# Attention with turned heads: values formed once and reordered by DMA, and an adapter's first matmul on two column tiles of TensorE

## The chip, the cores and the metric

The kernel runs on one core of one Trainium2 chip. The metric is the device time of one execution in microseconds (us). TensorE is called PE below (its weight loads PEld), VectorE DVE, ScalarE ACT, GpSimd POOL, and SyncE, which issues all DMAs here, SP.

## The reference, cut to what matters

The batch has 8 sequences of 512 tokens with 256 features, all in fp32. Each passes an attention block with 16 heads of 16 features, a feed-forward layer, an adapter, a rotation of feature pairs, and a second adapter.

```python
x = _ln(src) * (1.0 + scale) + shift                  # per batch, from the time step
q, k, v = (heads(x @ W + b) for W, b in ((Wq, bq), (Wk, bk), (Wv, bv)))
scores = q @ k.T / sqrt(16) + attention_bias          # (8, 16, 512, 512) of bias
probs = softmax(where(src_mask, -inf, scores))
x = x + (heads_joined(probs @ v) @ Wo + bo)
x = x + gelu2((_ln(x) * g2 + beta2) @ W1 + b1) @ W2 + b2

# an adapter, twice, with a rotation between the two; A = 64
hidden = gelu(x @ down_W.T + down_b)                  # (512, 256) -> (512, 64)
hidden = hidden @ expert_W[domain].T + expert_b[domain] + domain_emb[domain]
x = layer_norm(hidden @ up_W.T + up_b + x) * gamma + beta
```

## The kernel before

**The order of the work.** The kernel does not emit instructions as its loops run. `Plan` collects tasks, each with a cost per engine, a rank, and the buffers it reads and writes. `Plan.run` then plays them through a list scheduler: an engine that is free takes the ready task of the lowest rank for which buffers are left, and the tasks are emitted in that order. Where two engines can do a task (most PSUM evictions), the one that is free first takes it. A changed cost, buffer count or dependency therefore changes the order of all engines. Each engine then runs its own instructions strictly in the emitted order; so does SP with its DMA issues.

**Stages.** `prepare(b)` loads a sequence, normalises it, transposes it to `xT` (features on partitions) and forms q, k and v. `attention(u, n)` handles one unit: a batch, a group of four heads (`g`), and a tile of 128 queries; there are 128 units. `finish(b, ts)` takes two token tiles of 128 (in the very last half of the run, one at a time) through output projection, feed-forward and both adapters. While batch b is in attention, `prepare(b + 1)` and the `finish` of earlier halves are interleaved with it by rank.

**A unit.** Four bias tiles of 128x512 are loaded (L863), POOL adds the mask (L867), PE forms scores (L875), DVE adds them to the bias tile with the row minimum (L886), ACT takes the exponential in place (L890). The probabilities then have to get keys onto the partitions. There are two ways:

- Straight heads: PE transposes four blocks (L925) and ACT or DVE evicts them (L652) to `pT`.
- Turned heads: the first `TURNED = 2` heads of a group. DVE transposes 32x32 blocks (L901) to `tb`, and a DMA of four issues (L910) brings the blocks to `pT`. In this way the keys of a block of 128 land in a turned order: partition 4r + m holds key 32m + r. `turned_groups(b)` says which groups are turned: all four, but only the last one in batch 0 and only the first three in batch 7.

The product with the values (L951) runs on four column tiles of 32, one per head of the group, with 32 columns of `v_pad` from a head's start as weights. `v_pad` holds for each token tile and head 16 features and a one, which gives the softmax's sum.

**Values in two orders.** For the turned heads the values must stand on the partitions in the turned order. Before the change, `prepare` evicts each transposed half of the sequence twice, once to `xT` and once, permuted, to one of two buffers `xTp` that it borrows from the bias buffers (L760 on ACT, L762 on DVE). Each token tile's values are then formed in parts (L810): the turned heads of every group from `xTp`, the others from `xT`. In batches 0 and 7 there are three parts, else two, with two matmuls each. DVE adds the bias (L821).

**The adapter's way down.** `adapter` transposes two token tiles, and multiplies with the 64 columns of `down_W.T` (L1059): per half of the features one matmul with 64 weight columns and 256 tokens streamed, output on 64 partitions. ACT takes the gelu (L1065) to `hid`, whose 65th row is one. `db` holds the bias per batch.

Bias buffers: 17 (`BIAS`). An fp32 matmul leaves two records of weight load and two of matmul in the trace.

Of the kernel before, what the change touches and what calls it, by code (L numbers as in the profile page):

```python
# [219 lines left out]
def conditioned_sequence_kernel(  # L220
# [45 lines left out]
    QZ = slots("qz", 2, [P, 2, NC, S])  # L266
    KT = slots("kT", 2, [P, NC, S])
    VP = slots("v_pad", 2, [P, NT * H * (HD + 1) + 32 - HD - 1])
    BIAS = slots("bias", 17, [P, S])
    LOW = slots("low", 4, [P, 4])  # L270
    PT = slots("pT", 2, [P, 4 * NT * 2 * P])
    TB = slots("tb", 2, [P, TURNED * S])
# [60 lines left out]

    def heads_of(v):

        return v[:, : NT * H * (HD + 1)].rearrange("p (t h e) -> p t h e", t=NT, h=H)

    def turned_groups(b):

# [18 lines left out]
    invalid = const.tile([A, B], F32, tag="invalid", name="invalid")  # L358
    expert_i = const.tile([1, B], I32, tag="expert_i", name="expert_i")
    ccT = const.tile([P, NC, B + 1], F32, tag="ccT", name="ccT")  # L360
    db = const.tile([A, B + 1], F32, tag="db", name="db")
    ada_rows = tc.dram_tile([B, 2 * D], F32, name="ada_rows")
    rot_rows = tc.dram_tile([B, 2 * D], F32, name="rot_rows")
    turned_rows = tc.dram_tile([B, D], F32, name="turned_rows")
# [101 lines left out]
    def constants():  # L466
        plan.rank = -13.0

        further = Buffer(BG, lambda t: t[:, :8])
        plan(PE, 0.3, lambda: nc.tensor.matmul(  # L470
            further.t, shifted[:, :P], cols[:, :8], start=True, stop=True),
            [], [further], mode="full", at=4.0)

        def biases():
            nc.vector.tensor_tensor(
                bk,
                cols[:, C_BK : C_BK + NG].rearrange("p (c u) -> p c u", u=2)[:, :, 0],
                further.t[:, 4:8].rearrange("p (c u) -> p c u", u=2)[:, :, 1],
                ALU.add,
            )  # L480

            for u, src in enumerate((cols[:, C_BQ : C_BQ + NG], further.t[:, :4])):
                nc.vector.tensor_scalar(
                    bqh[:, u], src.rearrange("p (c u) -> p c u", u=2)[:, :, u],
                    halves[:, u : u + 1], None, ALU.mult,
                )

        plan(DVE, 0.6, biases, [further], ["bk", "bqh"], at=4.2)

        for c in range(NC):  # L490
            for n, w in ((1, wq), (2, wk)):

                def dense(n=n, w=w, c=c):
                    for k in range(NC):
                        src = first[:, n, k, c * 2 * P : (c + 1) * 2 * P]
                        src = src.rearrange("p (u j e) -> p u j e", u=2, e=32)[:, :, :, :HD]
                        dst = w[:, k, c, :].rearrange("p (j u d) -> p u j d", u=2, d=HD)
                        nc.gpsimd.tensor_copy(dst, src)

                plan.rank = -9.0 + 0.1 * (n + 2 * c)  # L500
                plan(POOL, 0.55, dense, [], [("w", n, c)], at=7.5 + 1.2 * n)


        for i, v_pad in enumerate(VP.tiles):

            def clear(v_pad=v_pad):
                nc.gpsimd.memset(v_pad, 0.0)
                nc.gpsimd.memset(heads_of(v_pad)[:, :, :, HD : HD + 1], 1.0)

            plan.rank = -10.0  # L510
            plan(POOL, 2.0, clear, [], [("ones", i)])
        plan.rank = 1.0

        def later():
            for hid in HID.tiles:
                nc.gpsimd.memset(hid[A:A1, :], 1.0)

        plan(POOL, 0.6, later, [], ["hid1"])

        plan(ACT, 0.25, lambda: nc.scalar.activation(  # L520
            b1s, cols[:, C_B1 : C_B1 + NF], AF.Copy, scale=0.851), [], ["b1s"], at=4.0)
# [25 lines left out]
    def rotations():  # L547
# [88 lines left out]
        plan(PE, 0.9, hidden, ["ccT", "wd"], [hs], mode="down")  # L636

        def added():
            nc.vector.tensor_scalar(
                db[:, :B], hs.t[:, 1, :B], cols[:A, C_DB + 1 : C_DB + 2], None, ALU.add  # L640
            )
            nc.vector.tensor_scalar(
                db[:, B:], hs.t[:, 0, B:], cols[:A, C_DB : C_DB + 1], None, ALU.add
            )

        plan(DVE, 0.3, added, [hs], ["db"])


    def evict(pair, r, w, act=0.47, dve=0.6):
# [78 lines left out]
    def prepare(b):  # L728
# [8 lines left out]
                m8.t, mask[b].rearrange("(t p) k -> p t k", p=P)), [], [m8], data=1.1)  # L737
        rstd = statistics(res, rk, range(NT), at=(4.0, 4.0, 4.8, 4.8) if b == 0 else None)
        normed(lambda t: res.t[:, t, :], rk, res, rk, range(NT), rstd)
        xT, xTp = Buffer(XT), [Buffer(BIAS) for _ in range(NC)]  # L740
        for c in range(NC):
            ps = Buffer(BG)

            def turn(c=c, ps=ps):
                for t in range(NT):
                    nc.tensor.transpose(
                        ps.t[:, t * P : (t + 1) * P], res.t[:, t, c * P : (c + 1) * P], ident
                    )

            plan(PE, 0.44, turn, rk, [ps], mode="full")  # L750

            def modulated(e, place, c=c, ps=ps):

                s, t = modc[:, c, b : b + 1], modc[:, NC + c, b : b + 1]
                dst, src = xT.t[:, c, :], ps.t
                if place:
                    dst = xTp[c].t.rearrange("p (k r m) -> p k m r", k=NT, m=4)
                    src = src.rearrange("p (k m r) -> p k m r", k=NT, m=4)
                if e == ACT:
                    nc.scalar.activation(dst, src, AF.Identity, bias=t, scale=s)  # L760
                else:
                    nc.vector.tensor_scalar(dst, src, s, t, ALU.mult, ALU.add)  # L762

            for place in range(2):
                plan({ACT: 0.66, DVE: 0.72 + 0.33 * place}, 0, lambda e, place=place, m=modulated: m(e, place),
                     [ps, "modc"], [xTp[c] if place else (xT, c)])

        qz, kT, v_pad = Buffer(QZ), Buffer(KT), Buffer(VP)

        def chunk(w, c, n):  # L770
            ps = Buffer(BG)
# [12 lines left out]
        for c in range(NC):  # L784
# [6 lines left out]
            if b == 0 and c == 0:  # L791

                plan.end(-8.0, -5.0)
                plan.begin()
        bv = bv_row.rearrange("p (h d) -> p h d", h=H)
        for h in range(2):
            ps = Buffer(BG, lambda t: t.rearrange("p (i d) -> p i d", i=2))
            for i in range(2):
                t = 2 * h + i

                def sums(t=t, i=i, ps=ps):

                    t0, t1 = turned_groups(b)
                    parts = (xTp, 0, t0, t1), (xT, 1, 0, NG), (xT, 0, 0, t0), (xT, 0, t1, NG)
                    for src, u, g0, g1 in parts:
                        if g0 == g1:
                            continue
                        for c in range(NC):
                            cut = "p (g u e) -> p u g e"
                            nc.tensor.matmul(  # L810
                                ps.t[:, i, :].rearrange(cut, g=NG, u=2)[:, u, g0:g1],
                                src[c].t[:, t * P : (t + 1) * P] if src is xTp
                                else xT.t[:, c, t * P : (t + 1) * P],
                                wv[:, c, :].rearrange(cut, g=NG, u=2)[:, u, g0:g1],
                                start=(c == 0), stop=(c == NC - 1),
                            )

                plan(PE, 0.87, sums, [(xT, 0), (xT, 1), *xTp, "wv"], [(ps, i)], mode="full")
            for i in range(2):
                t = 2 * h + i  # L820
                plan(DVE, 0.335, lambda t=t, i=i, ps=ps: nc.vector.tensor_tensor(  # L821
                    heads_of(v_pad.t)[:, t, :, :HD], ps.t[:, i, :].rearrange("p (h d) -> p h d", h=H),
                    bv, ALU.add), [(ps, 0), (ps, 1), ("ones", 0), ("ones", 1), "bv"], [(v_pad, t)])
        negs = [Buffer(NEG) for _ in range(NT)]
        for t in range(NT):
            plan(ACT, 0.52, lambda t=t: nc.scalar.activation(
# [17 lines left out]
        if b == 0:  # L844
            for n, task in enumerate(plan.stream):
                task.rank = 1.0 + n
            plan.stream = None
        state[b] = (res, rk, m8, negs, qz, kT, v_pad)


    pTs, sums_of, live = {}, {}, {}
# [1 line left out]
    def attention(u, n):  # L853
        b, g, qt = u
        c, par = divmod(g, 2)
        half, i = divmod(qt, 2)
        _, _, m8, negs, qz, kT, v_pad = state[b]
        qs = slice(qt * P, (qt + 1) * P)
        plan.rank = n - 2.0

# [81 lines left out]
        def values():  # L942
            for kc in range(NT):
                for j in range(4):
                    at = (kc * H + 4 * g + j) * (HD + 1)
                    if j < turned:
                        pj = pT.t[:, : 8 * TURNED * P].rearrange(
                            "p (a h k c) -> p h k a c", a=8, h=TURNED, k=NT)[:, j, kc]
                    else:
                        pj = pT.t.rearrange("p (j k f) -> p j k f", j=4, k=NT)[:, j, kc]  # L950
                    nc.tensor.matmul(  # L951
                        pv.t[32 * j : 32 * j + 32, :], v_pad.t[:, at : at + 32],
                        pj, start=(kc == 0), stop=(kc == NT - 1),
                    )

        plan(PE, 1.77, values,
             [(v_pad, t) for t in range(NT)]
             + [(pT, a, j) for a in range(2) for j in range(turned, 4)]
             + [(pT, a) for a in range(2) if turned], [pv], mode="col")
        sb = Buffer(PVS)  # L960
# [81 lines left out]
    def adapter(b, l, res, rk, ts):  # L1042
# [9 lines left out]
            eus[l] = eu  # L1052
        eu = eus[l]
        xT, xk = half_transposed(lambda t: res.t[:, t, :], rk, ts)
        ps, hid = Buffer(BG, lambda t: t[:A, : 2 * P]), Buffer(HID)

        def down():
            for c in range(NC):
                nc.tensor.matmul(  # L1059
                    ps.t[:, :w], wd[:, l, c, :], xT.t[:, c, :w], start=(c == 0),  # L1060
                    stop=(c == NC - 1),
                )

        plan(PE, 0.05 + 0.43 * n, down, [*xk, "wd"], [ps], mode="down")
        plan(ACT, 0.15 + 0.12 * n, lambda: nc.scalar.activation(  # L1065
            hid.t[:A, :w], ps.t[:, :w], AF.Gelu, bias=db[:, b : b + 1] if l else db[:, B:]),
            [ps, "hid1", "db"], [hid], mode="gelu")

        def add(ps):
            nc.vector.tensor_tensor(res.t[:, rows], ps, res.t[:, rows], ALU.add)  # L1070
# [267 lines left out]
```

## Time and profile before

| | |
|---|---|
| median of 3 runs | 959.73 us (958.97 to 961.05) |
| the profiled execution, its time | 959.75 us |
| its span, first to last instruction | 957.9 us |
| mean granted TensorE clock | 0.987 of full |
| DMA: share of the 16 engines, moved | 71.8%, 214.25 MB |
| chain that ended last, by engine | PE 59%, ACT 12%, DVE 10%, DMA 8%, POOL 7%, issue 4% |
| L810, matmuls of the values | 288 records |
| L1059, the adapters' way down | 136 records; 128x256 form 396 ns busy each |
| L760 to the turned order, ACT | 11 of 1282 ns |
| L762 to the turned order, DVE | 5 of 1230 ns |
| L1065 gelu, ACT | 30 of 64x256 at 469 ns, 4 of 64x128 at 362 ns |

The page gives each engine's busy time, the groups of instructions by line with a mean duration and the idle time before them with what ended it, and the chain of work followed back from the last instruction. A matmul's duration in a group contains the length of the pipeline; how long PE is really taken by it is seen from the start of the next one, as in the chain in order of time.

### The profile page before, as it was taken

To read this page: it belongs to the slowest core of one execution; us is meant where nothing else is said; L and a number is where in the kernel's file an instruction comes from. 1 tells how busy PE (TensorE), PEld (TensorE's weight loads), DVE (VectorE), ACT (ScalarE), POOL (GpSimd) and SP (SyncE) were. 2 spreads that over 40 slices of the span, in tenths; PEclk is the share of its full clock that TensorE was granted. 3 is DMA by queue.
4 is the path that set the end of the run, shared out by engine and by line. 5 is a ranking of instruction groups with operands and counts; after the bars stand their busy time and mean duration, and the time that the engine had idled before them with its cause. 6 is when DMAs were issued, how large, how long until landed. Compare 5 with 4: busy or idle time off the path is not lost.

```text
span 957.9 us, 20961 instructions
## 1 busy us (share of the span) xinstructions
PE 905.7 (95%) x6646; PEld 594.7 (62%) x6646; DVE 783.4 (82%) x2142; ACT 764.8 (80%) x1379; POOL 754.1 (79%) x841
## 2 busy tenths in 40 slices
PE   7989999999999999999999999999989999899994
PEld 5646666567566765667656666567656666566782
DVE  3778788887979898988978888888888888788656
ACT  5977779787897878979797888978799786897542
POOL 7699999787877879789796878888796987888122
PEclk8999999999999999999999999999999999999997
DMA  9497495888859876797958878597775968878000
GB/s 295 151 325 230 157 318 164 269 255 243 243 168 277 273 239 194 243 283 219 305 159 261 259 224 286 159 295 260 240 239 170 292 202 261 257 219 261 11 16 23
DMA packets 158945, 214.25 MB, mean 224 GB/s; under 512 B 18479, under 2 KB 90201, under 8 KB 158834
## 3 DMA queue, kind: packets, MB, share of 16 engines
q1 hardware_dynamic: 158834, 212.91, 71.8%
q8 instruction: 53, 0.87, 0.4%
q14 instruction: 58, 0.48, 0.1%
HBM read 149.89 MB, written 4.24 MB: 161 GB/s over the span
## 4 chain that ended last, share of the span: by engine, by line
PE 59%; ACT 12%; DVE 10%; DMA 8%; POOL 7%; issue 4%; SPq 1%; POOLq 0%; DVEq 0%; ACTq 0%
PE bank L875 10%; PE bank L1031 10%; PE bank L925 9%; PE bank L951 8%; PE bank L1006 8%; DMA bias<-in_bias 7%; POOL bias L867 4%; PE bank L773 4%; ACT bias L890 3%; DVE bias L886 3%; PE bank L1059 2%; PE bank L694 2%; PE bank L718 2%; PE bank L810 2%; ACT bank L682 1%
## 5 line engine op out<-in xcount | busy, mean ns | idle before, releaser
L867 POOL TENSOR_TENSOR bias<-bias,neg 128x512 f32<-128x512 f32 x512 | 580.8, 1161 | 101.1 <-DMA bias<-in_bias 73.4
L890 ACT ACTIVATE bias<-bias,low 128x512 f32<-128x512 f32 x512 | 343.6, 719 | 74.1 <-DVE low L886 73.6
L886 DVE CUSTOM_DVE_ANT_0 bias<-bank,bias 128x512 f32<-128x512 f32 x512 | 327.8, 684 | 71.2 <-PE bank L875 63.5
L925 PE MATMUL bank<-shifted,bias 128*128 128x128 f32 x1152 | 161.7, 278 | 11.5 <-ACT pT L652 2.3
L925 PEld LDWEIGHTS bank<-shifted,bias 128*128 128x128 f32 x1152 | 128.6, 141 | 64.2 <-issue 15.0
L901 DVE STREAM_TRANSPOSE tb<-bias 128x512 f32<-128x512 f32 x224 | 148.3, 691 | 9.4 <-ACT bias L890 8.8
L875 PE MATMUL bank<-kT,qz 32*128 32x512 f32 x1024 | 152.2, 643 | 0.6 <-DVE low L886 0.6
L652 ACT COPY pT<-bank 128x512 f32<-128x512 f32 x218 | 119.6, 583 | 22.3 <-PE bank L925 21.5
L1006 PE MATMUL bank<-hT,w 128*128 128x256 f32 (+1 forms) x544 | 123.8, 371 | 3.3 <-DVE gT L1022 1.8
L951 PE MATMUL bank<-pT,v_pad 128*32 128x256 f32 x2048 | 125.0, 385 | 0.6 <-DVE res L1124 0.3
L1031 PE MATMUL bank<-w,gT 128*128 128x256 f32 x496 | 122.3, 383 | 0.0
L1006 PEld LDWEIGHTS bank<-hT,w 128*128 128x128 f32 x544 | 95.2, 190 | 26.5 <-issue 8.4
L1031 PEld LDWEIGHTS bank<-w,gT 128*128 128x128 f32 x496 | 89.6, 190 | 26.7 <-issue 14.8
L951 PEld LDWEIGHTS bank<-pT,v_pad 128*32 128x32 f32 x2048 | 60.5, 110 | 60.9 <-issue 11.8
L1018 POOL TENSOR_SCALAR sig<-sig 128x512 f32<-128x512 f32 (+1 forms) x68 | 40.2, 593 | 55.3 <-ACT sig L1015 52.5
L875 PEld LDWEIGHTS bank<-kT,qz 32*128 32x128 f32 x1024 | 43.4, 183 | 43.7 <-issue 21.5
L1022 DVE SCALAR_TENSOR_TENSOR gT<-bank,cols,sig 128x256 f32<-128x256 f32 (+1 forms) x128 | 54.3, 465 | 14.2 <-POOL sig L1018 14.1
L1015 ACT ACTIVATE sig<-bank,b1s 128x256 f32<-128x256 f32 (+1 forms) x136 | 55.7, 456 | 8.2 <-PE bank L1006 7.9
L660 DVE BATCH_NORM_STATS2 st<-res 128x6 f32<-128x256 f32 x128 | 52.4, 410 | 10.1 <-DMA res<-in_x 8.5
L652 DVE COPY pT<-bank 128x512 f32<-128x512 f32 x70 | 46.4, 680 | 5.7 <-PE bank L925 4.7
L682 ACT ACTIVATE bank<-res,rstd 128x256 f32<-128x256 f32 x64 | 36.3, 567 | 16.9 <-POOL rstd L669 15.4
L668 POOL TENSOR_TENSOR rstd<-rstd,neg_half 128x2 f32<-128x2 f32 (+2 forms) x59 | 43.4, 736 | 4.9
(145 smaller groups left out, 1117.6 us busy)
## 6 DMA issues: line engine op xcount, KB each, us to landing
bias<-in_bias SPq DMA_DIRECT2D x512, 256.0 KB, 4.3
pT<-tb SPq DMA_DIRECT2D x448, 128.0 KB, 3.6
out<-res SPq DMA_DIRECT2D x15, 256.0 KB, 3.5
res<-in_x SPq DMA_DIRECT2D x7, 512.0 KB, 4.7
m<-in_mask SPq DMA_DIRECT2D x8, 256.0 KB
mod<-ada_rows SPq DMA_DIRECT2D x8, 256.0 KB
w<-in_w SPq DMA_DIRECT2D x2, 1024.0 KB
rot<-rot_rows SPq DMA_DIRECT2D x8, 256.0 KB, 4.2
```

The costliest lines, as they stand in the source:

```text
L652: nc.scalar.copy(*pair()) if e == ACT else nc.vector.tensor_copy(*pair())), r, w)
L867: plan(POOL, 1.12, lambda j=j: nc.gpsimd.tensor_tensor(dif[j].t, dif[j].t, negs[qt].t, ALU.add), [negs[qt]], [dif[j]])
L875: nc.tensor.matmul(sc[j].t, qz.t[strip, par, c, qs], kT.t[strip, c, :], start=True, stop=True,)
L886: plan(DVE, 0.61, lambda j=j: nc.vector.tensor_tensor_reduce(dif[j].t, sc[j].t, dif[j].t, -1.0, 3.0e38, ALU.add, ALU.min, low.t[:, j : j + ...
L890: plan(ACT, 0.61, lambda j=j: nc.scalar.activation(dif[j].t, dif[j].t, AF.Exp, bias=low.t[:, j : j + 1], scale=-1.0), [(low, j)], [dif[j]] ...
L901: plan(DVE, 0.62, lambda j=j: nc.vector.transpose(tb.t.rearrange("p (m h k c) -> h p k m c", m=4, h=TURNED, k=NT)[j], dif[j].t.rearrange(" ...
L925: nc.tensor.transpose(ps.t[:, kc, :], dif[j].t[:, kc * P : (kc + 1) * P], ident)
L951: nc.tensor.matmul(pv.t[32 * j : 32 * j + 32, :], v_pad.t[:, at : at + 32], pj, start=(kc == 0), stop=(kc == NT - 1),)
L1006: nc.tensor.matmul(ps.t[:, i, :w], w1[:, c, f * P : (f + 1) * P], hT.t[:, c, :w], start=(c == 0), stop=(c == NC - 1),)
L1015: plan(ACT, 0.155 + 0.1 * n, lambda i=i, f=f, ps=ps, sg=sg: nc.scalar.activation(sg.t[:, i, :w], ps.t[:, i, :w], AF.Tanh, bias=b1s[:, f : ...
L1022: plan(DVE, 0.14 + 0.13 * n, lambda i=i, f=f, ps=ps, sg=sg: nc.vector.scalar_tensor_tensor(gT.t[:, f, :w], ps.t[:, i, :w], cols[:, C_B1 + ...
L1031: nc.tensor.matmul(ps.t[:, i, :], gT.t[:, f, i * P : (i + 1) * P], w2[:, f, :], start=(f == 0), stop=(f == NF - 1),)
```

## The change

Values are formed once per token tile, from `xT` alone, with two matmuls of 256 columns. The second, permuted eviction and the buffers `xTp` are gone. `v_pad` is laid out by the head's place in its group first, so that the part of the turned heads is one contiguous run of 544 numbers on each partition. When all four token tiles of a batch are in, SP issues four DMAs that copy that run to a new buffer `v_turn`, each from 32 neighbouring partitions to every fourth one. The values' product takes its weights of the turned heads from `v_turn`. There are two `v_turn` buffers, and 16 bias buffers instead of 17.

In the adapter, each matmul of two token tiles is cut in two of 128 tokens, the second on the array's second 64 columns, so that its output lies on partitions 64 to 127. The gelu is taken in two instructions of 64x128, the second of which reads partitions 64 to 127 and writes partitions 0 to 63. `db` is therefore formed on both halves of the partitions. The planner's cost of the way down falls from 0.91 to 0.52, that of the gelu rises from 0.39 to 0.54.

```diff
-    BIAS = slots("bias", 17, [P, S])
+    VT = slots("v_turn", 2, [P, NT * NG * TURNED * (HD + 1) + 32 - HD - 1])
+    BIAS = slots("bias", 16, [P, S])
...
-        return v[:, : NT * H * (HD + 1)].rearrange("p (t h e) -> p t h e", t=NT, h=H)
+        return v[:, : NT * H * (HD + 1)].rearrange("p (j t g e) -> p t j g e", j=4, t=NT, g=NG)
...
-            for place in range(2):
-                plan({ACT: 0.66, DVE: 0.72 + 0.33 * place}, 0, lambda e, place=place, m=modulated: m(e, place),
-                     [ps, "modc"], [xTp[c] if place else (xT, c)])
+            plan({ACT: 0.66, DVE: 0.72}, 0, modulated, [ps, "modc"], [(xT, c)])
...
-                    parts = (xTp, 0, t0, t1), (xT, 1, 0, NG), (xT, 0, 0, t0), (xT, 0, t1, NG)
...
+                    for c in range(NC):
+                        nc.tensor.matmul(
+                            ps.t[:, i, :], xT.t[:, c, t * P : (t + 1) * P], wv[:, c, :],
+                            start=(c == 0), stop=(c == NC - 1),
+                        )
...
+        def turned_values():
+            size = NT * NG * TURNED * (HD + 1)
+            to = v_turn.t.rearrange("(r m) f -> m r f", m=4)
+            for m in range(4):
+                nc.sync.dma_start(to[m, :, :size], v_pad.t[32 * m : 32 * m + 32, :size])
+
+        plan(DMA, 1.8, turned_values, [(v_pad, t) for t in range(NT)], [v_turn], data=1.0)
...
-                        pv.t[32 * j : 32 * j + 32, :], v_pad.t[:, at : at + 32],
+                        pv.t[32 * j : 32 * j + 32, :],
+                        (v_turn if j < turned else v_pad).t[:, at : at + 32],
...
         def down():
             for c in range(NC):
-                nc.tensor.matmul(
-                    ps.t[:, :w], wd[:, l, c, :], xT.t[:, c, :w], start=(c == 0),
-                    stop=(c == NC - 1),
+                for i in range(n):
+                    nc.tensor.matmul(
+                        ps.t[A * i : A * i + A], wd[:, l, c, :], xT.t[:, c, i * P : (i + 1) * P],
+                        start=(c == 0), stop=(c == NC - 1),
+                    )
+
+        def hidden():
+            for i in range(n):
+                lanes = slice(A * i, A * i + A)
+                nc.scalar.activation(
+                    hid.t[:A, i * P : (i + 1) * P], ps.t[lanes], AF.Gelu,
+                    bias=db[lanes, b : b + 1] if l else db[lanes, B:],
                 )
...
-        plan(PE, 0.05 + 0.43 * n, down, [*xk, "wd"], [ps], mode="down")
+        plan(PE, 0.52, down, [*xk, "wd"], [ps], mode="down")
+        plan(ACT, 0.27 * n, hidden, [ps, "hid1", "db"], [hid], mode="gelu")
```

The DVE addition L821 now writes 4x4x16 numbers per token tile instead of 16x16, and POOL clears the last 15 columns of both `v_turn` buffers at the start.

## The prediction

> **What bounds the kernel now.** I read the page's busy shares first, then the busy time by stage, then the chain in order of time, then the groups of the touched lines, then SP's own queue.
>
> From the page (busy us, share of the span, instructions):
>
> ```profile
> span 957.9 us, 20961 instructions
> PE 905.7 (95%) x6646; PEld 594.7 (62%) x6646; DVE 783.4 (82%) x2142; ACT 764.8 (80%) x1379; POOL 754.1 (79%) x841
> ```
>
> PE's ends are modelled, so 95% alone proves little. The busy time by stage (first number the stretch's length, then PE, PEld, DVE, ACT, POOL) shows the same in stretches of about one batch:
>
> ```profile
> 312.00:432.00 120.00, 115.03 (x866) 76.81 (x866) 106.49 (x287) 100.07 (x177) 98.56 (x106) 1.00 0.78 244
> ...
> 552.00:672.00 120.00, 116.43 (x817) 76.28 (x818) 101.61 (x279) 103.65 (x181) 98.68 (x105) 1.00 0.78 242
> ...
> 890.00:958.00 68.00, 53.33 (x348) 40.70 (x342) 41.76 (x116) 28.54 (x69) 16.95 (x42) 0.92 0.05 16
> ```
>
> In a steady batch PE lacks only 3.6 to 5 of 120 us; the next engine, DVE, lacks 13 or more. PE is the bound, at full granted clock, except at the start and in the last 40 us. What a matmul really occupies is its pitch, which the chain in order of time gives (start, length, engine, line, records; an fp32 matmul leaves two records). From the start and from batch 2:
>
> ```profile
> 28.19 1.31 PE bank L810 x12
> ```
>
> ```profile
> 182.93 0.44 PE bank L925 x4
> ...
> 191.71 1.86 PE bank L951 x32
> ...
> 199.65 0.89 PE bank L810 x8
> 200.54 0.88 PE bank L718 x4
> ...
> 213.94 1.01 PE bank L1059 x4
> ...
> 259.80 1.22 ACT bias L760
> ...
> 262.63 1.18 ACT bias L760
> ```
>
> Four records that stream 128 columns take 0.44 us (0.109 each); four of 256 columns take 0.87 to 0.88. L1059, the adapters' way down, is 0.87 plus 0.14 of changing the tiling of the array. L951 streams 256 columns on four column tiles: 32 records in 1.86 us is 58 ns each against 217 alone, so four tiles run at once at 3.7 of 4. The last two rows are the copy of the modulated rows into the turned order, on the chain.
>
> **The change part by part.**
>
> *Adapters' way down.* 30 calls on two token tiles: four records of 256 columns become eight of 128, in two column tiles of 64. If the tiles run together as in L951, that is four steps of 0.109, 0.44, and with the switch 0.58 us instead of 1.01: 0.43 saved, 30 × 0.43 = 12.9 us of PE. The four calls on one token tile keep four records of 128 columns: nothing. The weight loads decide whether this holds; in the groups (busy us, mean ns | idle before and its releasers):
>
> ```profile
> L925 PEld LDWEIGHTS bank<-shifted,bias 128*128 128x128 f32 x1152 | 128.6, 141 | 64.2 <-issue 15.0 <-ACT bias L890 11.5 <-ACT pT L652 7.1
> ...
> L951 PEld LDWEIGHTS bank<-pT,v_pad 128*32 128x32 f32 x2048 | 60.5, 110 | 60.9 <-issue 11.8 <-ACT bias L890 10.0 <-DVE res L1070 2.6
> ...
> L1059 PEld LDWEIGHTS bank<-hT,wd 128*64 128x64 f32 x136 | 16.2, 140 | 18.9 <-issue 3.3 <-DVE hT L652 3.2 <-ACT hT L652 2.5
> ```
>
> Eight loads of 140 ns now stand in four steps of 109. [...] L951's 32 loads of 110 ns are 3.5 us inside 1.86 us, on column tiles of the same rows, and L925's loads of 141 ns pass at a pitch of 109. I take 0.43 saved; [...].
>
> *Values.* Before, the four matmuls of a token tile in batches 1 to 6 take 0.89; after, two of 256 columns at L718's 0.87: 24 tiles × 0.02 = 0.5 us. In batches 0 and 7 a token tile has six matmuls, 1.31: 8 × (1.31 − 0.87) = 3.5. Together 4.0 us of PE. PE's sum is 16.9.
>
> *The turned copies go.* 11 on ACT at 1282 ns and 5 on DVE at 1230: 14.1 us of ACT and 6.2 of DVE. 8 of ACT's stand on the chain (9.7 us). They also held the PSUM bank and two bias buffers.
>
> *Gelu in two.* A 64x256 ACTIVATE is 469 ns, a 64x128 one 362 (row L1065): 30 × (2 × 362 − 469) = 7.7 us more on ACT, which still nets −6.4. The second half reads lanes 64 to 127 and writes lanes 0 to 63; no row shows such a shift, bounds 362 and 469 each, I take 362. On a layer's own chain down and gelu together are 0.43 − 0.26 = 0.17 shorter. Table loads stay at 56 in the instruction order, so the planner did not scatter the gelus; changes of PE tiling go from 397 runs to 398.
>
> *v_pad's layout.* The 32 DVE additions now write 4x4x16 instead of 16x16. Runs stay 16 elements; the row is 412 ns; a transposing one such as L762's costs 1230 against 800. Bounds 0.41 and 0.63 (the same ratio), taken 0.41: zero, and at most 7 us on DVE, which has 13 us a batch to spare. Two more 64-lane additions for db, and two POOL memsets of 15 columns at the start, are below 1 us in all, beside the start's loads.
>
> *The transfer of the turned values.* 32 DMAs of 32 partitions × 2176 B. Its nearest row is pT<-tb:
>
> ```profile
> bias<-in_bias SPq DMA_DIRECT2D x512, 256.0 KB, 4.3
> pT<-tb SPq DMA_DIRECT2D x448, 128.0 KB, 3.6
> ```
>
> Four issues of pT<-tb take 2.50 us of SP (0.62 each), so SP gets 2.5 us a batch more, and the DMA engines 2.2 MB on 214 (1%, at a share of 72%). Landing about 3.6 us. Who waits: the values' matmuls of the next batch's first head group. In the trace of before, v_pad of batches 1 to 7 is full 28 to 48 us ahead of them (batch 7: 778.1 and 819.8), and batch 0 is turned only in its fourth group (39.8 and 82.4). So 2.5 + 3.6 fits. Queued behind the wait on SP are bias loads and pT<-tb, and behind those POOL. In the changed kernel's instruction order, the bias load behind the transfer is for a buffer that DVE frees after the last v_pad write (batches 2, 4, 6, 7) or one instruction ahead of it (3); in batch 0 v_pad is done before SP gets there; only in batches 1 and 5 does SP wait for v_pad alone. So the wait is hidden by what SP waits for anyway, in its own queue:
>
> ```profile
> SPq L863 <- DVE tb L901: 86.8, 58, 7.7
> SPq L863 <- PE bank L925: 73.1, 56, 6.9
> ```
>
> If that cover is gone, a batch pays up to the 2.5 us of issue. I take nothing, with 0 and 8 × 2.5 = 20 us as bounds.
>
> *Bias buffers 17 to 16.* The two turned copies took two of 17 from the copy to the last values' matmul, 505 of 958 us, so 15 were left for half the time and 17 for the other. POOL's gaps ahead of L867 are as dense in the one (48 us in 505) as in the other (44 in 452). Nothing, from either side ±2 us.
>
> **Sum.** PE does 16.9 us less. How much reaches the end? If only the chain's PE share (59%) counted, 10; if all as in the steady stages (96%), 16. ACT and DVE, the other parts of the chain, get 6.4 and 6.2 us lighter, so I take 0.8: 13.5 us. The profiled execution takes 959.75 us (span 957.9 and 1.85 around it), the median of the runs 959.73, so both bases agree: 959.7 − 13.5 = 946.2. Planning the order anew moves unrelated waits, by a few us either way (PE's idle in a batch already differs by 1.6 us from stage to stage): own range 940 to 952.
>
> **Rivals.**
>
> *Other engines hold the end (12%).* PE gets shorter, but the loop bias load, POOL, DVE, ACT keeps its length: bias<-in_bias is 7% of the chain and POOL L867 4%. For it: POOL 99 us and DVE up to 106 of 120. Against: PE's own idle is the smallest. Half arrives: 952.
>
> *The column tiles don't run together (6%), so the change doesn't do what it says.* The call stays at 8 × 0.109 + 0.14 = 1.01. Left are the values, 4.0 × 0.8: 956.5. Against it, L951.
>
> *The transfer blocks SP (5%).* The 2.5 us of issue come on the path in half of the batches: 10 us given back, 956.
>
> *Loads are exposed (7%), the case that is slower.* Place: each way down of two token tiles. [...] It decides from the point where a call takes over 1.01 + 4.0/30 = 1.14 us, that is 70 ns exposed per load. For it: a load takes 140 ns, a step 109, and two loads fall in a step. Against: L925's and L951's pitches.
>
> **How the numbers follow.** The forecast has 70%. Faster by over 0.2% (1.9 us, about what a measurement of this kernel can tell): the forecast, the half gain, and most of the 956 cases, 0.89; within 0.2%: 0.04, the rest of those; slower 0.07. The range 939 to 956.5 takes in all but the exposed loads and the outer ends of the forecast.
>
> **What would show it.** Right: L1059's successor takes 0.58 us in the chain with both halves' records starting within some ns; 0.87 a token tile for the values in every batch; ACT and DVE each about 6 us less busy; PE busy near 889; PE's idle per batch still 3 to 5 us. SP's wait at the new transfer short or in place of a bias wait. Wrong: a way down over 0.8 us, PE's idle above 6 us per batch, L951 waiting for v_turn, or POOL's wait for bias loads well over 73 us.

## The result, and the profile after

The changed kernel takes 949.96 us (median of 14 runs, 944.99 to 957.14) against 959.6 us of the kernel before beside it (14 runs): a ratio of 0.9888, interval 0.9861 to 0.9916. That is 10.7 us by the ratio, which compares runs taken side by side, and 9.6 between the medians. The profiled execution took 954.41 us, the second longest of its runs, at a mean granted clock of 0.977 (before: 0.987).

The page of the changed kernel: span, busy time of each engine, and the chain by engine.

```profile
span 952.6 us, 20975 instructions
...
PE 901.4 (95%) x6606; PEld 595.6 (63%) x6606; DVE 785.1 (82%) x2143; ACT 760.7 (80%) x1394; POOL 754.5 (79%) x843
...
PE 53%; ACT 20%; DVE 9%; DMA 9%; issue 4%; SPq 2%; POOL 2%; DVEq 0%; POOLq 0%; ACTq 0%
```

PE is busy 4.3 us less, not 16.9, and its idle time is 51.2 us against 52.2. Part of this is the clock. In some stretches the granted clock is 0.50; counted as span × (1 − granted clock), this half clock cost 12.5 us in the profiled execution before and 21.9 us in this one, so at full clock PE would be about 13.7 us less busy (an estimate from these two and the 4.3). On the chain PE's share went from 59% to 53% and ACT's from 12% to 20%. The stretches of one batch (length, then PE, PEld, DVE, ACT, POOL, granted clock, DMA share, GB/s):

```profile
312.00:432.00 120.00, 114.31 (x860) 75.77 (x859) 105.56 (x286) 101.00 (x182) 99.92 (x110) 0.99 0.77 244
552.00:672.00 120.00, 117.34 (x875) 76.17 (x873) 104.12 (x283) 103.79 (x186) 98.78 (x106) 1.00 0.78 245
885.00:953.00 68.00, 54.49 (x369) 43.75 (x368) 41.53 (x113) 31.52 (x79) 17.64 (x43) 0.87 0.05 17
```

PE lacks 5.7 us in the one and 2.7 us in the other. The two edited stages, in the chain in order of time (start, length, engine, line, records):

```profile
197.19 0.59 PE bank L1062 x8
197.78 0.59 PE bank L700 x4
198.37 0.87 PE bank L925 x8
199.24 0.87 PE bank L803 x4
```

L1062 is the way down of two token tiles: eight records in 0.59 us where four took 1.01. L803 is a token tile's values: 0.87 us. So both edits do on PE what they say. Groups of the changed lines (busy us, mean ns | idle before and its releasers):

```profile
L1070 ACT ACTIVATE hid<-bank,db 64x128 f32<-64x128 f32 x64 | 23.2, 363 | 5.6 <-PE bank L1062 4.6
...
L724 PEld LDWEIGHTS bank<-eu,hid 65*128 65x128 f32 x128 | 22.5, 193 | 16.5 <-ACT hid L1070 12.7 <-issue 1.0 <-ACT res L688 0.8
L1062 PEld LDWEIGHTS bank<-hT,wd 128*64 128x64 f32 x256 | 15.0, 140 | 13.7 <-ACT hT L658 5.1 <-issue 1.9 <-ACT bias L890 1.2
...
L811 DVE TENSOR_TENSOR v_pad<-bank,bv_row 128x256 f32<-128x256 f32 x32 | 13.4, 420 | 4.0 <-PE bank L803 3.2
```

The gelu's halves take 363 ns each, the shifted one included, and the new layout of `v_pad` costs 1.3 us in all (13.4 against 12.1 busy). The second row is the matmul after the gelu: its weight load waits 12.7 us for `hid`, 6.6 us in the kernel before (17 times against 9).

### The profile page after: what moved, and what is told of

Same layout as the page of the kernel before. It is cut to its first block, busy times and chain, and to the rows that moved or that the text cites. A ratio compares the mean times of both kernels' runs of the same rounds, so it can differ in the third digit from the quotient of the medians.

```text
span 952.6 us, 20975 instructions
## 1 busy us (share of the span) xinstructions
PE 901.4 (95%) x6606; PEld 595.6 (63%) x6606; DVE 785.1 (82%) x2143; ACT 760.7 (80%) x1394; POOL 754.5 (79%) x843
## 4 chain that ended last, share of the span: by engine, by line
PE 53%; ACT 20%; DVE 9%; DMA 9%; issue 4%; SPq 2%; POOL 2%; DVEq 0%; POOLq 0%; ACTq 0%
PE bank L925 8%; PE bank L1032 8%; PE bank L875 8%; PE bank L951 8%; PE bank L1007 6%; ACT bias L890 6%; PE bank L772 4%; DMA bias<-in_bias 4%; DMA pT<-tb 3%; PE bank L724 3%; DVE bias L886 2%; PE bank L803 2%; PE bank L700 2%; ACT pT L658 2%; DVE tb L901 2%
## 5 line engine op out<-in xcount | busy, mean ns | idle before, releaser
L890 ACT ACTIVATE bias<-bias,low 128x512 f32<-128x512 f32 x512 | 339.8, 719 | 51.4 <-DVE low L886 50.6
L875 PE MATMUL bank<-kT,qz 32*128 32x512 f32 x1024 | 156.0, 640 | 2.5 <-DVE low L886 1.9
L901 DVE STREAM_TRANSPOSE tb<-bias 128x512 f32<-128x512 f32 x224 | 147.6, 691 | 10.7 <-ACT bias L890 9.2
L658 ACT COPY pT<-bank 128x512 f32<-128x512 f32 x213 | 117.4, 583 | 42.6 <-PE bank L925 39.2
L1007 PE MATMUL bank<-hT,w 128*128 128x256 f32 (+1 forms) x544 | 125.6, 376 | 5.9 <-ACT pT L658 5.6
L1007 PEld LDWEIGHTS bank<-hT,w 128*128 128x128 f32 x544 | 97.2, 192 | 29.3 <-issue 7.9
L951 PE MATMUL bank<-pT,v_turn 128*32 128x256 f32 x896 | 108.9, 385 | 4.1 <-DMA pT<-tb 4.1
L951 PEld LDWEIGHTS bank<-pT,v_turn 128*32 128x32 f32 x896 | 48.3, 110 | 56.0 <-issue 14.3
L666 DVE BATCH_NORM_STATS2 st<-res 128x6 f32<-128x256 f32 x128 | 52.4, 410 | 13.5 <-DMA res<-in_x 11.8
L951 PEld LDWEIGHTS bank<-pT,v_pad 128*32 128x32 f32 x1152 | 55.2, 110 | 8.3 <-issue 1.9
L658 DVE COPY pT<-bank 128x512 f32<-128x512 f32 x75 | 50.1, 681 | 7.4 <-PE bank L925 7.3
```

The lines of the kernel that those rows point to most:

```text
L658: nc.scalar.copy(*pair()) if e == ACT else nc.vector.tensor_copy(*pair())), r, w)
L875: nc.tensor.matmul(sc[j].t, qz.t[strip, par, c, qs], kT.t[strip, c, :], start=True, stop=True,)
L890: plan(ACT, 0.61, lambda j=j: nc.scalar.activation(dif[j].t, dif[j].t, AF.Exp, bias=low.t[:, j : j + 1], scale=-1.0), [(low, j)], [dif[j]] ...
L901: plan(DVE, 0.62, lambda j=j: nc.vector.transpose(tb.t.rearrange("p (m h k c) -> h p k m c", m=4, h=TURNED, k=NT)[j], dif[j].t.rearrange(" ...
L951: nc.tensor.matmul(pv.t[32 * j : 32 * j + 32, :], (v_turn if j < turned else v_pad).t[:, at : at + 32], pj, start=(kc == 0), stop=(kc == N ...
L1007: nc.tensor.matmul(ps.t[:, i, :w], w1[:, c, f * P : (f + 1) * P], hT.t[:, c, :w], start=(c == 0), stop=(c == NC - 1),)
```

## The experiments

Ratios are to the kernel before on the same chip, with 95% intervals; 0.1% is about 1 us. Line numbers of the variants shift by a few.

**Each half alone.** `v_only` is the change's diff without the part on `down` and `hidden`: the values' half and the transfer, with before's adapters; `d_only` is that part alone, with its new planner costs; `d_order` the same instructions as `d_only`, but with the planner told before's costs, so that every engine keeps the order of the kernel before.

```diff
 # d_order: the adapters' edits, and
-        plan(PE, 0.52, down, [*xk, "wd"], [ps], mode="down")
-        plan(ACT, 0.27 * n, hidden, [ps, "hid1", "db"], [hid], mode="gelu")
+        plan(PE, 0.05 + 0.43 * n, down, [*xk, "wd"], [ps], mode="down")
+        plan(ACT, 0.15 + 0.12 * n, hidden, [ps, "hid1", "db"], [hid], mode="gelu")
```

> The values' half of the change alone: values formed once and the turned heads' brought over by the transfer, 16 bias buffers; the adapters' way down and gelu as before. Measured in the changed kernel, the values' matmuls give PE back 3.0 us, and ACT and DVE lose 20 us of permuted copies. Theory 'PE bound': 2 to 5 us faster than before, 955 to 958. Theory 'the transfer blocks SP' (8 x 2.5 us of issue, landing 6.6 us once on the chain): same or slower, 960 to 965. Theory 'the new order decides': anything within 6 us of before, unrelated to the PE time saved.

> The adapters' half alone: way down of two token tiles on two column tiles and gelu in two; values in two orders and 17 bias buffers as before. PE gets 12.5 us back (1.008 to 0.588 us a call). Theory 'PE bound': 0.7 of it arrives, 950 to 952. Theory 'the transfer blocks SP': without the transfer this half gains more than the whole change did, 944 to 947. Theory 'the new order decides': no relation to the 12.5 us, 945 to 958.

> As the adapters' half alone, but the planner is told the old costs (0.91 for the way down, 0.39 for the gelu), so that every engine's order is that of the kernel before and only the instructions of the two steps differ. Theory 'PE bound': the same gain as with the new order, 950 to 952, with way down at 0.59 us. Theory 'the new order decides': the PE time saved turns into waits in an order made for other costs, 955 to 960.

Measured: `v_only` 0.9965 (0.995 to 0.9981), `d_only` 0.9973 (0.9959 to 0.9988), `d_order` 1.0001 (0.9986 to 1.0017). The chain of `d_order` has the way down at 0.59 us, and yet nothing is won. Its page and two of its stages:

```profile
span 958.4 us, 21233 instructions
...
PE 898.6 (94%) x6766; PEld 594.2 (62%) x6766; DVE 785.0 (82%) x2144; ACT 772.4 (81%) x1409; POOL 753.8 (79%) x841
```

```profile
312.00:432.00 120.00, 114.57 (x894) 76.97 (x890) 108.21 (x290) 102.29 (x183) 100.50 (x109) 1.00 0.78 247
552.00:672.00 120.00, 113.89 (x822) 75.66 (x825) 101.20 (x276) 102.34 (x181) 97.33 (x104) 0.99 0.79 241
```

PE is busy 7.1 us less than before and idle 7.6 us more; ACT is busy 7.6 us more. Against before's 116.43, PE does 113.89 us in the second stretch and no more of the program passes. Followed task by task, POOL's mask additions stay within 3 us of their times in the kernel before all along: the time taken off PE does not add up. Where some of it goes is in the waits of the weight loads (engine, line, waited for: us in total, times, longest). Of `d_order`:

```profile
PEld bank L720 <- ACT hid L1071: 14.6, 21, 1.9
```

Of the kernel before:

```profile
PEld bank L718 <- ACT hid L1065: 6.6, 9, 1.6
```

Not all of these 8 us hold PE up (the matmuls behind the loads wait 5.0 us against 3.8), but the direction is plain: PE is ready sooner, and ACT, which now takes two instructions, gives `hid` no sooner. `d_order` thus changes two things at once, 12.5 us less on PE and 7.7 us more on ACT, and the result is the sum of both.

**The transfer away.** `no_move` leaves the 32 DMAs out and keeps the order.

```diff
         def turned_values():
-            for m in range(4):
-                nc.sync.dma_start(to[m, :, :size], v_pad.t[32 * m : 32 * m + 32, :size])
+            return
...
-                        (v_turn if j < turned else v_pad).t[:, at : at + 32],
+                        v_pad.t[:, at : at + 32],
```

> The whole change without the transfer: SP issues none of the 32 DMAs, the values' product of turned heads reads v_pad instead (that part of the output is computed with rows in the wrong order); order of all other instructions unchanged. Theory 'PE bound': as the whole change within 2 us, 948 to 951. Theory 'the transfer blocks SP': 4 to 8 us faster than the whole change, 942 to 946, with fewer gaps on PE.

Measured: 0.9867 (0.9842 to 0.9892). Beside the whole change that is 0.0021, 2.0 us for the transfer, with intervals that overlap. Where it can bite, the changed kernel's own trace shows once. SP's queue there, and then the chain of that stretch:

```profile
661.19 2.75 SPq L821 DMA_DIRECT2D v_turn<-v_pad  x4
664.27 0.33 SPq L863 DMA_DIRECT2D bias<-in_bias  x1
665.01 3.32 SPq L910 DMA_DIRECT2D pT<-tb  x4
668.43 0.54 SPq L863 DMA_DIRECT2D bias<-in_bias  x1
```

```profile
661.19 6.58 DMA v_turn<-v_pad
667.78 0.55 SPq L910
...
668.43 2.85 DMA bias<-in_bias
...
671.42 1.16 POOL bias L867
...
676.29 3.68 PE bank L1007 x8
```

The transfer lands 6.58 us after its first issue, by the chain. SP's last issue of `pT<-tb` starts 0.01 us after that, the bias load behind it lands late, POOL's addition follows, and through POOL's and ACT's next work PE stands still for 2.14 us. In the other batches it is not on the chain.

**The way down serial again, in the whole change's order.** `serial` computes two token tiles one after the other on the first 64 columns, with two gelus; `serial_one` does that with one gelu of 64x256.

```diff
-            for c in range(NC):
-                for i in range(n):
+            for i in range(n):
+                for c in range(NC):
                     nc.tensor.matmul(
-                        ps.t[A * i : A * i + A], wd[:, l, c, :], xT.t[:, c, i * P : (i + 1) * P],
+                        ps.t[:, i * P : (i + 1) * P], wd[:, l, c, :], xT.t[:, c, i * P : (i + 1) * P],
...
 # serial_one, besides
-            for i in range(n):
-                lanes = slice(A * i, A * i + A)
-                nc.scalar.activation(
-                    hid.t[:A, i * P : (i + 1) * P], ps.t[lanes], AF.Gelu,
...
+            nc.scalar.activation(
+                hid.t[:A, :w], ps.t[:, :w], AF.Gelu, bias=db[:A, b : b + 1] if l else db[:A, B:]
+            )
```

> The whole change with its order, but the way down of two token tiles stays on one column tile: eight records of 128 columns one after the other, 1.01 us instead of 0.588, gelu still in two instructions. 12.5 us of PE time come back, nothing else moves. Theory 'PE bound': 9 to 12 us slower than the whole change, 959 to 962. Theory 'ACT and DVE share the bound' (the adapters' half alone gave 2.6 us, and nothing in the old order): 0 to 4 us slower, 950 to 954.

> As 'serial', with the gelu of two token tiles again in one ACTIVATE, so ACT has 7.7 us less than in the whole change and PE 12.5 us more. Work per engine is that of the values' half alone (957.3 us); only the order, planned with the costs 0.52 and 0.54, is the whole change's. Theory 'PE bound': within 1 us of 'serial', 958 to 961. Theory 'ACT and DVE share the bound': 3 to 5 us faster than 'serial'. Theory 'the new order decides': well away from 957, on the side of the whole change, 950 to 953.

Measured: `serial` 0.9908 (0.9875 to 0.994), `serial_one` 0.9892 (0.9853 to 0.9932). Neither can be told from the whole change at 0.9888. The chain of `serial` has the call back at its old length:

```profile
375.87 1.02 PE bank L1062 x8
```

and its page shows PE busier and less idle than with the column tiles:

```profile
span 950.1 us, 20975 instructions
...
PE 905.8 (95%) x6606; PEld 604.1 (64%) x6606; DVE 784.3 (83%) x2143; ACT 757.0 (80%) x1394; POOL 753.2 (79%) x843
```

30 calls are dearer by 0.43 us on PE, and the time by 0.0020 or 1.9 us, which the intervals do not tell from nothing. `serial` and the whole change have the same order on every engine and the same instructions on ACT, so this is the one pair in which PE's work alone differs. Put together, the two intervals leave room for up to about 6 us; 0.8 of 12.5 would be 10. So the column tiles are not what makes most of the whole change's gain.

**ACT's part.** `d_half` is `d_order` without the second gelu; what it leaves uncomputed is filled with ones at the start.

```diff
-                nc.gpsimd.memset(hid[A:A1, :], 1.0)
+                nc.gpsimd.memset(hid, 1.0)
...
         def hidden():
-            for i in range(n):
+            for i in range(1):
```

> The adapters' half in the old order, with the second gelu of each pair left out (the second token tile's hidden values are not computed), so that ACT loses 10.9 us against 'd_order' and is 3.2 us below before. Theory 'ACT shares the bound': the PE time saved now arrives, 951 to 955. Theory 'the order decides': still 958 to 961, since PE's waits sit at DVE and DMA.

Measured: 0.9932 (0.9903 to 0.996), 0.69% or 6.6 us below `d_order` (3.5 to 9.7 with both intervals), for 10.9 us of ACT (30 instructions of 363 ns). In this order a microsecond off the gelu is worth about 0.6 us. Against the kernel before, `d_half` has 12.5 us less of PE and 3.2 us less of ACT and gains 6.5 us. At that rate ACT's 3.2 us would bring only 1.9, so part of PE's saving seems to arrive once ACT is not made dearer: the zero of `d_order` is no proof that PE's time is worth nothing. How much each is worth alone in the old order was not measured.

**A later transfer.** `late_move` issues the four parts one by one, in the last two units ahead of the batch.

```diff
-        plan(DMA, 1.8, turned_values, [(v_pad, t) for t in range(NT)], [v_turn], data=1.0)
...
+        if n % 16 >= 14 and b + 1 < B:
+            plan.rank = n - 0.5
+            for m in range(2 * (n % 16 - 14), 2 * (n % 16 - 14) + 2):
+                transfer[b + 1](m, [(low, 2 * (m % 2) + 1)])
```

> The whole change with the transfer of the turned values of batches 1 to 7 taken apart: four tasks of one issue each, given to SP in the last two units before the batch, between bias loads, instead of four issues in a row right behind the v_pad writes. Theory 'the transfer blocks SP': as without a transfer, 945 to 948. Theory 'the transfer costs nothing': as the whole change, 949 to 951.

Measured: 0.9954 (0.9933 to 0.9976): meant to win the 2 us back, it loses 6. The tasks' order came out new on all engines, so it says nothing of the transfer, but it does say what a new order can cost.

**Order against work.** Four kernels hold one and change the other. `after_old` is the whole change with before's planner costs, and its order is that of `v_only`; `costs_only` is before's work planned with the new costs; `after_true` is the whole change with costs near the measured times; `nudge` is the kernel before with a cost raised by 0.02.

```diff
 # after_old
-        plan(PE, 0.52, down, [*xk, "wd"], [ps], mode="down")
-        plan(ACT, 0.27 * n, hidden, [ps, "hid1", "db"], [hid], mode="gelu")
+        plan(PE, 0.05 + 0.43 * n, down, [*xk, "wd"], [ps], mode="down")
+        plan(ACT, 0.15 + 0.12 * n, hidden, [ps, "hid1", "db"], [hid], mode="gelu")
 # costs_only: before's work with PE 0.52, ACT 0.27 * n, DVE 0.5 for db
 # after_true
-        plan(PE, 0.52, down, [*xk, "wd"], [ps], mode="down")
-        plan(ACT, 0.27 * n, hidden, [ps, "hid1", "db"], [hid], mode="gelu")
+        plan(PE, 0.49, down, [*xk, "wd"], [ps], mode="down")
+        plan(ACT, 0.363 * n, hidden, [ps, "hid1", "db"], [hid], mode="gelu")
 # nudge
-        plan(PE, 0.05 + 0.43 * n, down, [*xk, "wd"], [ps], mode="down")
+        plan(PE, 0.07 + 0.43 * n, down, [*xk, "wd"], [ps], mode="down")
```

> All instructions of the whole change, but the planner is told the old costs of the adapters; the order is that of the values' half alone (957.3 us) in all engines but for the two edited steps. Theory 'PE bound': the 12.5 us of PE saved in the way down arrive at 0.7, 947 to 950. Theory 'the new order decides': as the values' half alone, 955 to 958, as d_order came out as before.

> The kernel before with not one instruction's work changed: only the planner's costs of the adapters are those of the changed kernel (way down 0.52, gelu 0.27 per tile, db 0.5), so that it orders anew. Theory 'PE bound' or any theory of work: 960, as before, or slower because the plan is now wrong by 0.4 us a call. Theory 'the new order decides': the order's part of the gain appears without any work saved, 951 to 956.

> The whole change, the planner's costs of the two steps set to what the trace shows (way down 0.49 plus its mode switch of 0.1, gelu 0.363 a tile): a third order for the same work. Theory of work: within 2 us of the whole change, 948 to 952. Theory 'the new order decides': anywhere from 945 to 958.

> The kernel before, the planner's cost of the way down raised by 0.02, work unchanged: a measure of what a new order alone does. Theory of work: within 1 us of before, 959 to 961. Theory 'the new order decides': moves by 3 us or more to either side.

Measured: `after_old` 0.9959 (0.9942 to 0.9976), `costs_only` 0.9999 (0.9981 to 1.0017), `after_true` 0.9892 (0.9866 to 0.9918), `nudge` 1.0022 (1.0006 to 1.0039). With the runs above they fill a table of work against planner costs:

| work | planned with before's costs | with the change's costs |
|---|---|---|
| as before | 1 | 0.9999 (`costs_only`) |
| adapters' half | 1.0001 (`d_order`) | 0.9973 (`d_only`) |
| values' half | 0.9965 (`v_only`) | 0.9892 (`serial_one`) |
| both | 0.9959 (`after_old`) | 0.9888 (the change) |

Down a column, the adapters' half keeps the order (rows 1 to 2, and 3 to 4). It brings nothing with before's costs (+0.01%; −0.06%) and at most 0.26% with the new ones. The values' half (rows 1 to 3) brings 0.35% in the left column and 1.07% in the right; it has other tasks and so always a new order, and its work and its order cannot be told apart. Across, the costs alone are worth nothing to before's work, 0.28% to the adapters' half, and 0.7% (about 7 us) once the values are formed in the new way; between `after_old` and the change, which have the same instructions in two orders, the intervals do not touch, nor do they between `v_only` and `serial_one` (there the way down is in four matmuls instead of two, 1.02 us against 1.01). The order takes in which of ACT and DVE does an eviction: of the copies, ACT has 290 and DVE 131 in `after_old`, 295 and 126 in the change. `nudge` gives the size of what an order can do by chance: 0.22% for a cost changed by 20 ns, and `late_move` 0.66% against the whole change.

That about 7 us of the gain sit in the order is shown; why the new costs find a good order only on the values' half's work is not. Two neighbouring sets of costs (0.52 and 0.27, 0.49 and 0.363) make two different orders with the same time, which speaks against the luck of a single order, without ruling luck out. Not tried: 17 bias buffers beside `v_turn`, or 16 in the kernel before. None of these kernels that does the whole work is faster than the change.

## Why the prediction was right or wrong

The number came out near (946.2 forecast, 950.0 measured, inside the forecast's own 940 to 952), but mostly by another way than its sum, so that its nearness is in good part luck. The rival "other engines hold the end" describes the runs better: PE gets shorter and the work around it keeps its length; which engine holds it is not settled. (Half of 16.9 us makes 951.3; the forecast writes 952.)

**Right: what the edits cost on their own engine.** The way down was put at 0.58 us; from start to start it is 0.588 (median of 29 calls; 1.008 before), and over all calls PE gets 12.5 us back, forecast 12.9. The weight loads do not stand in the way: eight of 140 ns, 1.12 us in sum, pass within a call of 0.588 us on two column tiles of the same rows, and the row of all 256 has 15.0 us busy for 35.8 in sum, so the loads overlap each other too. The rival on exposed loads falls with this. So does the one on tiles that don't run together: in the trace the records of the two tiles start 6 to 7 ns apart. The values gave 3.0 us of 4.0 in the profiled execution, in which one pair of token tiles fell into half clock and took 2.98 us where the other pairs take about 1.82. The gelu's 363 ns were as taken, and `v_pad`'s layout 1.3 us where zero was taken.

**Wrong: "PE is the bound", and the factor 0.8.** The step that failed is that 0.8 of the PE time saved reaches the end, 13.5 of 16.9 us. Where PE's work alone differs (`serial` and the change), 12.5 us off PE brought 1.9, with room for about 6, where 0.8 would be 10. The adapters' half as a whole, with its 7.7 us more on ACT, brought −0.1, 0.6, 2.5 and 0.4 us in four orders held fixed (`d_order` against before, `after_old` against `v_only`, `d_only` against `costs_only`, the change against `serial_one`). Both edits under before's costs brought 3.9 us, of which `v_only` alone has 3.4.

Where the time went can be followed in the profiled executions. From before to `d_order`, PE's busy time without what half clock added fell by 11.9 us; idle time took 7.6 of it and half clock 4.8. From `serial` to the change it fell by 14.0; idle time took 6.9 and half clock 9.6 (granted clocks 0.987 and 0.977). The share of half clock is in large part that of the two executions: by the medians of all runs it costs 14.4 us before, 16.3 in `d_order`, 17.1 in `serial` and 18.0 in the change. The forecast had no term for this: it read the clock as full but for the start and the last 40 us, while half clock also fell near 830 us before, and after the change it costs 3.6 us more.

A lack of 3.6 to 5 us in 120 was read as "no other engine is in the way". But each engine's order is written down at build time, and PE's small gaps sit behind waits on ACT and DVE that hardly move when PE is shorter: in `d_order` POOL's mask additions, and the matmuls of the scores with them, kept their times within 3 us.

**Wrong: ACT as a side account.** The two gelus were netted against the copies (−6.4 us) and held to be off the path but for 0.17 us per layer. `d_half` puts 10.9 us of ACT at 6.6 us of time, by which the extra 7.7 would cost about 4.6 (an estimate). ACT may well be where the adapters' half lost its gain in the old order; PE's 12.5 us would then have been worth about 4.6 there, which is still far from 0.8. In the whole change's order this could not be separated (`serial` to `serial_one`, overlapping). Nor did both engines become 6 us lighter: ACT is 4.1 us less busy, and DVE 1.7 more. Its 6.2 us of turned copies were refilled in part, as the engine that is free first takes an eviction (before, then after):

```profile
L652 DVE COPY pT<-bank 128x512 f32<-128x512 f32 x70 | 46.4, 680 | 5.7 <-PE bank L925 4.7
...
L658 DVE COPY pT<-bank 128x512 f32<-128x512 f32 x75 | 50.1, 681 | 7.4 <-PE bank L925 7.3
```

**Mis-sized: the order.** "Planning the order anew moves unrelated waits, by a few us either way" stood in the forecast as noise about a gain from PE. With the change's work it was the largest term: the same instructions take 0.71%, or 6.8 us, less in the order planned with the new costs than in the one planned with before's. The work of before gains nothing from the same costs (`costs_only`).

**The transfer.** Four issues took 2.42 to 3.25 us of SP per batch, 2.5 forecast. The cost was taken as nothing within 0 to 20; `no_move` puts it at about 2 us, not separable from nothing. The landing was taken at 3.6 us; the one that reached the chain took 6.58. The values' matmuls never waited for `v_turn` in the trace. The cover named, waits that SP has anyway, is still there in the changed kernel:

```profile
SPq L863 <- DVE tb L901: 80.9, 61, 8.5
SPq L863 <- PE bank L925: 78.8, 52, 8.9
```

**16 bias buffers.** POOL's wait for bias loads was a sign to watch, and it rose from 73.4 us:

```profile
POOL bias L867 <- DMA bias<-in_bias: 86.2, 70, 4.4
```

But it is 73.8 in `after_old` and 74.4 in `after_true`, with 16 buffers as well, and 83.6 without the transfer: it goes with the order and is no sign of the time, as `after_true` is as fast. Of the buffers' number alone no run tells.

**The signs.** Fulfilled: 0.58 and 0.87 us, ACT lighter. Not fulfilled: PE busy near 889 (901.4, of which 9.4 us are what half clock took beyond the execution before). PE's idle of 3 to 5 us per batch (2.7 and 5.7) decided nothing, since the idle in a stretch of fixed length is blind to how much work passes in it.

## What to carry to other kernels

A busy share of 95%, even 97% in the steady stage, does not make an engine the bound when all engines run in a fixed order: take work off it with the order held, and look whether the end moves, before you count the saving. Where a planner uses costs, an edit and its cost are two changes; measure them apart, and take an order's luck (here 0.2 to 0.7%) into the range as a term of its own. Price what the edit adds on the quieter engines too: leaving out 10.9 us of ACT brought 6.6 us here (`d_half`), and 12.5 us off PE alone about 1.9 (`serial` and the change), each in its own order.

## What the hardware showed beside this

Half clock often came after a short stretch in which PE stood still, in seven of the eight places named below for 1.57 to 3.83 us. Two places of the changed kernel's PE timeline (start, length, line, tiles, records [idle before, releaser]), with matmuls at half speed after the gap:

```profile
152.92 0.33 PE L700 MATMUL bank<-shifted,tmp 128*128 128x128 f32 x1 [1.57 <-ACT tmp L688]
...
153.88 3.50 PE L772 MATMUL bank<-xT,wk 128*128 128x512 f32 x4
...
676.29 3.68 PE L1007 MATMUL bank<-hT,w 128*128 128x256 f32 x8 [2.14 <-ACT pT L658]
```

Eight records of L1007 take 3.68 us where four take 0.87 elsewhere, and four of L772 3.50 where two take 0.86. Between the start and the last 25 us, such stretches lie near 59 (6.8 us long), 154, 321, 547, 676 and 823 us in the changed kernel (3.4 us each), and near 62 and 830 us in the kernel before. In both traces the stretches at one clock between two changes last 3.41 us or whole multiples of it (half clock 3.41 or 6.83, full clock from 3.41 to 764.6, which is 224 times 3.413). The length of a gap alone does not tell what follows: gaps of 1.76 us (before) and 1.59 us (after) brought no half clock. PE's busy time in the 3.41 us ahead of a change tells more. Three pairs of neighbouring windows of that length in the changed kernel, with edges whole multiples of it away from the changes of the clock (window, length, busy time of PE, PEld, DVE, ACT, POOL, granted clock, DMA share, GB/s):

```profile
150.78:154.20 3.42, 1.69 (x11) 1.07 (x10) 2.42 (x10) 3.07 (x6) 3.17 (x6) 1.00 0.85 239
154.20:157.61 3.41, 3.41 (x6) 1.35 (x5) 1.96 (x6) 3.41 (x8) 3.41 (x4) 0.50 0.77 276
447.70:451.11 3.41, 1.82 (x10) 1.45 (x10) 3.18 (x8) 2.74 (x7) 1.44 (x2) 1.00 0.86 257
451.11:454.53 3.42, 3.42 (x22) 2.25 (x21) 3.42 (x10) 3.42 (x7) 1.83 (x3) 1.00 0.90 275
543.31:546.73 3.42, 3.05 (x8) 0.88 (x6) 3.39 (x11) 3.39 (x8) 3.21 (x5) 1.00 0.94 268
546.73:550.14 3.41, 3.41 (x16) 3.12 (x16) 3.31 (x11) 2.05 (x4) 3.41 (x4) 0.50 0.75 255
```

In the windows ahead of the stretches near 59, 154, 321, 676 and 823 us PE was busy for 0.88 to 1.69 of 3.41 us, before those of the kernel before for 1.12 and 1.21. After 1.82 us (second pair), and after 1.82 near 341 us in the kernel before, the clock stayed full. The third pair, with 3.05 us busy, does not fit, nor does a stretch at 932 us after 1.96, so this is what seven stretches have in common and no rule.

This is also a part of the spread: over 14 runs of the changed kernel, its time and the time lost to half clock go together (correlation 0.77), and its median granted clock is 0.981 against 0.985 in the runs of the kernel before beside the experiments, about 3.6 us more lost. Whether fewer gaps would bring these back was not tried.
